# Order of loads, flushes and far updates in the recurrence of a four-layer graph kernel on one core

## The chip, the core and the metric

The kernel runs on one NeuronCore of a Trainium2 chip. A core has five engines, each with its own queue of instructions in program order: TensorE (PE, with its weight loads PEld), VectorE (DVE), ScalarE (ACT), GpSimd (POOL) and SyncE (SP, which here only issues DMA transfers). The metric is the device time of one execution in microseconds; lower is better.

## The reference

The input is x of 64 graphs x 256 nodes x 256 features and a weighted adjacency matrix per graph. Four layers follow each other, each of the form x = layernorm(x + layer(x, adj)). The change is in layer 0, a recurrence over the nodes, in which all 64 graphs go side by side:

```python
d = jnp.sum(adj, axis=-1)
dinv = jnp.where(d != 0, 1.0 / jnp.where(d != 0, d, 1.0), 0.0)
norm_adjT = jnp.swapaxes(adj, 1, 2) * dinv[:, :, None]

def step(h, i):
    x = jnp.take(h_e, i, axis=1)
    row = jnp.take(norm_adjT, i, axis=1)
    x_par = jnp.einsum('bj,bjd->bd', row, h)
    iou = x @ W_ioux.T + b_ioux + x_par @ W_iouh.T + b_iouh
    r, z = jnp.split(iou, 2, axis=1)
    r, z = (jax.nn.sigmoid(r), jax.nn.sigmoid(z))
    hc = jnp.tanh(x @ W_coux.T + b_coux + x_par * r @ W_couh.T + b_couh)
    h_new = z * x_par + (1.0 - z) * hc
    h = jax.lax.dynamic_update_slice(h, h_new[:, None, :], (0, i, 0))
    return (h, None)
h_out, _ = jax.lax.scan(step, h_e, jnp.arange(n))
```

Node i needs the sum x_par over all nodes j: for j < i with the new states h, for j >= i with the old ones, which are x itself. The 256 steps cannot run side by side. Layers 1 to 3 are a graph convolution, a masked attention and a masked attention with eight heads, done graph by graph.

## The kernel before

**Setup.** The function `_recurrence` first computes, for the first 128 nodes, the part of x_par that comes from old states (the loop over `g` in steps of `GB` = 8 graphs, products in `x_product`, VectorE's copies, stores into the DRAM tensor `Us` in `x_out`). Weights are loaded and turned in between. The input tiles `xX` are loaded from ACT's queue (L139), `xA` from SP's (L138). Then the pools of setup are given back, and the pools `stream`, `work` and `ps` take their memory: a tile of those pools waits until the old users of its memory are done. After this come the first S table (`chain_S(0)`), the raw table for late sums (`late_load(0)`), the first x (`load_x`, SP) and the first three blocks of sums (`sums_in`, ACC from `Us`).

**A node.** The main loop runs over the nodes n, written out by hand: the order of the calls is the order on each engine, and no scheduler moves them. i = n % 32 is the row in a block of T = 32 nodes, p = n % 8 the place in a group of U = 8. A tile of 128 x 128 holds a state: 2 feature halves x 64 graphs on the partitions. The chain of a node is: transpose of xp on TensorE and ScalarE's copy into xpT; the products of r and z with xpT (`h_part`, L615); ScalarE's sigmoid rs (L839); transpose and product into rT; the products of c; tanh (L876); then on VectorE zcc (L878) and the next xp (L881). `state` (L661, L663) writes the new state twice, into PSUM (`keep`) and into SBUF (`hs`).

**How a new state reaches later nodes.** Each node's sum lies in the tile ACC of its group. The state of node n-1 must be added, times an entry of S, to the nodes up to the end of the next group:
- near targets by VectorE, one instruction each (`push`, L640). They stand in a list sorted by target; one or more for node n+1 come first, then up to 5 (`push(5)`), then up to 3 late in the node (`push(3)`, ahead of zcc);
- the last `FAR[p]` targets by GpSimd (`push_far`, a product into the tile `far`, L678, and a sum into ACC, L682), in the same node. At place 0 `behind` adds two more such pairs of 4 targets for the group after;
- everything further away by matrix products over many states at once. `late` (L531) reads the ring `Hw` of the last 64 states and goes through the DRAM tensor `Lb` into `late_sb`, which GpSimd adds at places 6 and 7 (L891). `early` (L424) reads states and adjacency from DRAM (`Hs`, `A`) and goes through `Es` into `early_sb`, added at places 3 and 4 (L833). `x_side` does the same for old states of the second 128 nodes, through `Us`.

GpSimd also makes `ready` (L820), which the next xp needs. Results of these products leave PSUM by ScalarE copies that stand in the list `copies`: one is taken at a node's start and two at its end (`next_of`). The output tile `ub` (copies xu and eu, L256) has two buffers in `stream`.

**Transfers.** All transfers in the loop are issued by SP, in this order in a node: states into the ring (`into_ring`, places 4 to 7, two states of two transfers each); two loads from a list ordered by rank (`next_load`, places 0 to 3); the transfers that earlier steps put on this node (`transfers`: stores to `Us`, `Es`, `Lb`, the receipt of `late_sb`); `early_sb` (place 0), ACC (place 1), x (place 2); the flush of ring rows to the DRAM tensor `Hd` (at rows 10 and 16); and what `degrees` does for the next block. `degrees` is a generator that is advanced at 14 given rows: four loads of 4 x 2 adjacency rows, two reductions on VectorE (L304) after each, then the inverse and the spread to `dinv`.

Of the kernel before, what the change touches and what calls it, by code (L numbers as in the profile page):

```python
# [9 lines left out]
F32 = mybir.dt.float32  # L10
# [9 lines left out]
P = 128  # L20
# [50 lines left out]
def _recurrence(tc, ident, Hd, x, adj, W_ioux, b_ioux, W_iouh, b_iouh, W_coux, b_coux, W_couh, b_couh, wide, then):  # L71
# [27 lines left out]
    XB = 4  # L99
    NG = B // 4  # L100
    HB = B // 2
    FAR = (2, 4, 4, 4, 4, 4, 3, 4)

    with ExitStack() as ctx:
        const = ctx.enter_context(tc.tile_pool(name="r_const", bufs=1))
# [467 lines left out]

        def load_x(a):

            xq = stream.tile([P, U // 2, D], F32, tag="xq", name=f"xq_{a}")
            for h in range(2):
                at = a * U + h * U // 2
                nc.sync.dma_start(xq[h * B:(h + 1) * B], x[:, at:at + U // 2, :])
            return xq  # L580

        def flip_x(a, e, xq):
# [89 lines left out]

        def push_far(j, hs, first, count):

            acc, s = cell(j, first, count)
            tmp = work.tile([P, 4, P], F32, tag="far", name=f"far_{j}_{first}", bufs=1)
            shape = [P, count, P]
            nc.gpsimd.tensor_mul(  # L678
                tmp[:, 0:count, :], hs.unsqueeze(1).to_broadcast(shape),
                s.unsqueeze(2).to_broadcast(shape),  # L680
            )
            nc.gpsimd.tensor_add(acc, acc, tmp[:, 0:count, :])  # L682

        tables = {k: {} for k in range(NB)}
        sums = {}
# [9 lines left out]
        with tc.tile_pool(name="r_first_ps", bufs=4, space=bass.MemoryType.PSUM) as xps:  # L695
            for g in range(0, B, GB):
                A, Xs = first_in.pop(0)
                nc.gpsimd.tensor_mul(
                    A[:, 0], A[:, 0], tri.unsqueeze(1).to_broadcast([P, GB, P])
                )  # L700
                for n in range(0, GB, 4):
                    ub = fst.tile([P, 4, D], F32, tag="ub", name=f"xu_{g}_{n}")
                    for e in range(0, 4, 2):
                        pb = xps.tile([P, 2, D], F32, tag="x", name=f"xp_{g}_{n}_{e}")
                        for q in range(2):
                            b = n + e + q
                            x_product(
                                pb, q, [A[:, jc, b, :] for jc in range(2)],
                                [Xs[jc][:, b, :] for jc in range(2)],
                            )  # L710
                        nc.vector.tensor_copy(ub[:, e:e + 2, :], pb)
                    x_out(0, g + n, ub)
                if g + 2 * GB < B:
                    first_in.append(first_load(g + 2 * GB))
                if g == 0:
                    load_weights()
                if g == 3 * GB:
                    turn_weights()
                if g == 2 * GB:
                    deg = fst.tile([P, T // 2], F32, name="deg_0", bufs=1)  # L720
                    nc.vector.tensor_reduce(deg, rows_0, AX.X, ALU.add)
                    inverse(deg, fst.tile([P, T // 2], F32, name="deg0_0", bufs=1))
                    dinv_from(deg, 0)
# [3 lines left out]
        work = ctx.enter_context(tc.tile_pool(name="r_work", bufs=2))  # L727
        ps = ctx.enter_context(tc.tile_pool(name="r_ps", bufs=1, space=bass.MemoryType.PSUM))

        tables[0]["Sd"] = chain_S(0)  # L730
        tables[0]["An"] = late_load(0)
        xq = {a: load_x(a) for a in range(2)}
        for a in range(3):
            sums_in(a)
        for e in range(2):
            flip_x(0, e, xq[0])
# [7 lines left out]
                x_part(G, 0, kc, gates)  # L744

        keep = ps.tile([P, 4, P], F32, tag="keep", name="keep")
        xp = new("xp", 0)
        nc.vector.tensor_scalar(xp, sums[0][:, 0, :], dinv[:, 0:1], None, ALU.mult)

        zcc = hs = None  # L750
        late_side = background = None
        behind = []
        x_left = x_side()
# [18 lines left out]
        for now in range(N):  # L772
# [4 lines left out]

            xpT = flip(xp, "xpT", n)
            next_of(copies, n)

            far = []
            if n:

                assert all(j == n - 2 for _, j in pushes)
                hs = state(n - 1)
                end = min((n - 1) // U * U + 2 * U, N)
                to = list(range(n + 1, end))
                near = to[:len(to) - min(FAR[p], len(to) - 1)] if to else []
                far = to[len(near):]
                pushes += [(m, n - 1) for m in near]  # L790
                pushes.sort()
                if p == 0:

                    behind = [(n - 1, hs, m, 4) for m in range(end, min(end + U, N), 4)]

                if p > 3 or n >= N - U:
                    for _ in range(min(2, len(ring_in))):
                        into_ring()
# [23 lines left out]
                    dinv[:, n + 1:n + 2].to_broadcast([P, P]),  # L822
                )
            push(5)
            if far:
                push_far(n - 1, hs, far[0], len(far))
            if behind:
                push_far(*behind.pop(0))
            if p in (3, 4):
# [35 lines left out]
            if not last:  # L865
                Sd = tables[kk]["Sd"][:, ii:ii + 1]
                v = keep[:, 3, :]
                nc.vector.scalar_tensor_tensor(v, zx, Sd, ready, ALU.mult, ALU.add)
                push(3)
                for kc in range(2):  # L870
                    x_part(rc, n + 1, kc, slice(0, 2))
                z = ps.tile([P, P], F32, tag="z", name=f"z_ps_{n + 1}")
                nc.scalar.copy(z, bias_z)
                for kc in range(2):
                    x_part(z, n + 1, kc, 2)
# [1 line left out]
            zcc = new("zcc", n, 1)  # L877
            nc.vector.tensor_mul(zcc, zc, c)  # L878
            if not last:
                xp = new("xp", n + 1)  # L880
                nc.vector.scalar_tensor_tensor(xp, zcc, Sd, v, ALU.mult, ALU.add)  # L881
            for _ in range(2):
                next_of(copies, n)
            if p < 4:
                for _ in range(2):
                    next_load(n)

            if p in (6, 7) and n + 8 - p in sides:
                half = slice(0, U // 2) if p == 6 else slice(U // 2, U)
                part = sums[n // U + 1][:, half]  # L890
# [8 lines left out]
                sums_in(n // U + 3)  # L899
            if p == 2 and n // U + 2 < N // U:  # L900
                xq[n // U + 2] = load_x(n // U + 2)
            if i == 10:
                flush(n - 26, n - 10)
            if i == T // 2:
                state_out(n - 1, hs)
                flush(n - T // 2, n - 1)
# [19 lines left out]
        while ring_in:  # L926
            into_ring()
# [618 lines left out]
```

## Time and profile before

| what | value |
|---|---|
| median of 3 runs | 3314.0 us (3300.75, 3314.0, 3314.47) |
| the profiled execution, own time | 3314.75 us |
| its span | 3313.0 us |
| mean granted TensorE clock | 0.973 |
| TensorE busy | 3077.3 us, 93% of the span |
| VectorE / ScalarE / GpSimd busy | 2630.6 / 1834.0 / 1925.8 us |
| share of TensorE in the chain that ended last | 79% |
| L640, near updates on VectorE | 1712, 478.6 us busy |
| L682 and L678, far updates on GpSimd | 313 each, 372.4 and 304.9 us busy |
| L839, the sigmoid rs on ScalarE | 256, 277 ns each |

The span is the time from the first to the last instruction of the profiled execution. Busy times of different engines overlap. In the timeline a row is: start and length in us, engine, line, operation, output and inputs, shape, count, and in brackets the idle time before it with what ended it. In a table of waits a row is: engine and line, what it waited for, total us, times, longest.

### The profile page before, as it was taken

The page shows a single profiled execution, that of the slowest core. Times are in us where ns is not written, and L with a number is a line of the kernel's source. Part 1 is how long each engine was busy: PE and PEld are TensorE (multiplying, and loading weights), DVE is VectorE, ACT ScalarE, POOL GpSimd, SP SyncE. Part 2 cuts the span into 40 slices and gives each one's busy share as a digit, 9 for nine tenths or more (in the row PEclk, how much of TensorE's full clock was granted, in tenths as well). Part 3 has the DMA queues.
Part 4 walks back from the last instruction along what each step waited for, and adds up shares of the span by engine and source line. Part 5 has one row for each costly group of instructions (what it writes and reads, how often), then busy time and mean ns, then how long its engine had stood idle before and what let it go on. Part 6 is the DMA issues. An engine that isn't in the chain of part 4 may idle for free.

```text
span 3313.0 us, 80062 instructions
## 1 busy us (share of the span) xinstructions
PE 3077.3 (93%) x28332; PEld 2275.4 (69%) x28332; DVE 2630.6 (79%) x7511; ACT 1834.0 (55%) x4690; POOL 1925.8 (58%) x2230
## 2 busy tenths in 40 slices
PE   4798979999989998977999999999999999999997
PEld 3565656565555555545888888888888888888885
DVE  3476767887777878865888888888888888888885
ACT  0154535554545544534666666666666666666664
POOL 2366667777667878843555555555555555555543
PEclk8899989999999999998999999999999999999999
DMA  9865557686867675424333333333333333333310
GB/s 295 250 163 132 156 144 178 157 194 166 202 166 179 152 180 136 118 58 94 76 77 78 78 78 78 76 81 77 76 79 79 77 78 77 78 77 78 77 43 20
DMA packets 806730, 385.73 MB, mean 116 GB/s; under 512 B 525260, under 2 KB 774232, under 8 KB 802648
## 3 DMA queue, kind: packets, MB, share of 16 engines
q1 hardware_dynamic: 788632, 363.66, 45.3%
q10 hardware_dynamic: 17696, 16.91, 1.6%
q8 instruction: 227, 3.72, 0.5%
q14 instruction: 175, 1.43, 0.1%
HBM read 261.75 MB, written 99.61 MB: 109 GB/s over the span
## 4 chain that ended last, share of the span: by engine, by line
PE 79%; DMA 8%; DVE 7%; issue 2%; SPq 2%; ACT 2%; POOL 1%; DVEq 0%; ACTq 0%; POOLq 0%
PE mm L1023 14%; PE rc L615 7%; PE rc L607 4%; PE s L1249 4%; PE mm_3v L1023 4%; PE mm_2f L1023 4%; PE late L531 3%; PE mm_2v L1023 3%; PE mm_3f L1023 3%; PE mm_t L1023 3%; PE mm_g L1023 3%; PE mm_2w L1023 3%; PE mm_2s L1023 3%; PE o L1284 3%; DVE ACC L640 3%; PE z_ps L615 2%
## 5 line engine op out<-in xcount | busy, mean ns | idle before, releaser
L1261 POOL TENSOR_TENSOR p3s<-p 128x256 f32<-128x256 f32 x512 | 359.2, 735 | 271.2 <-ACT p L1259 271.0
L640 DVE SCALAR_TENSOR_TENSOR ACC<-keep,S,ACC 128x128 f32<-128x128 f32 x1712 | 478.6, 343 | 14.2 <-POOL ACC L891 8.6
L1023 PE MATMUL mm<-xT,weights 128*128 128x256 f32 x2048 | 484.1, 385 | 2.7 <-ACT xT L1139 2.7
L1023 PEld LDWEIGHTS mm<-xT,weights 128*128 128x128 f32 x2048 | 386.3, 191 | 80.2 <-ACT xT L1139 28.8
L682 POOL TENSOR_TENSOR ACC<-ACC,far 128x384 f32<-128x384 f32 (+1 forms) x313 | 372.4, 1190 | 24.5
L1258 DVE TENSOR_TENSOR p<-s,neg 128x512 f32<-128x512 f32 x512 | 317.7, 683 | 85.6 <-PE s L1249 85.6
L979 ACT ACTIVATE y<-y,shift,rstd 128x256 f32<-128x256 f32 x512 | 279.7, 596 | 156.3 <-DVE shift L977 156.2
L1259 ACT ACTIVATE p<-p 128x512 f32<-128x512 f32 x512 | 307.1, 629 | 3.5 <-DVE p L1258 3.0
L678 POOL TENSOR_TENSOR far<-hs,S 128x384 f32<-128x384 f32 (+1 forms) x313 | 304.9, 974 | 4.7
L820 POOL TENSOR_TENSOR ready<-ACC,dinv 128x128 f32<-128x128 f32 x255 | 102.2, 401 | 316.1 <-DVE ACC L640 315.6
L607 PE MATMUL rc<-WxT,xqT 128*64 128x256 f32 x2048 | 276.2, 392 | 0.0
L971 POOL TENSOR_TENSOR rstd<-rstd,mhalf 128x2 f32<-128x2 f32 x256 | 173.8, 697 | 133.4 <-DVE rstd L970 131.6
L1298 DVE RECIPROCAL rT<-o 128x256 f32<-128x256 f32 x128 | 223.7, 1748 | 0.0
L967 DVE BATCH_NORM_STATS2 st<-y 128x6 f32<-128x256 f32 x512 | 209.6, 409 | 12.6 <-POOL y L1160 9.7
L615 PE MATMUL rc<-WhT,xpT 128*64 128x128 f32 x2048 | 170.7, 288 | 43.1 <-ACT xpT L624 40.3
L839 ACT ACTIVATE rs<-rc 128x128 f32<-128x128 f32 x256 | 70.9, 277 | 247.5 <-PE rc L615 247.5
L1160 POOL TENSOR_TENSOR y<-y,g 128x512 f32<-128x512 f32 x64 | 81.3, 1270 | 215.2 <-ACT g L1157 195.3
L615 PE MATMUL rc<-WhT,rT 128*64 128x128 f32 x2048 | 172.9, 291 | 33.6 <-DVE rT L843 33.1
L615 PEld LDWEIGHTS rc<-WhT,rT 128*64 128x64 f32 x2048 | 109.5, 139 | 131.8 <-DVE rT L843 111.7
L1171 ACT ACTIVATE qk<-mm,weights 128x256 f32<-128x256 f32 x256 | 107.3, 470 | 161.2 <-PE mm L1023 159.6
L615 PEld LDWEIGHTS rc<-WhT,xpT 128*64 128x64 f32 x2048 | 107.9, 137 | 124.2 <-ACT xpT L624 112.9
L531 PE MATMUL late<-Hw,An 64*32 64x256 f32 x3840 | 165.4, 396 | 25.6 <-DMA A<-in_adj_dram 9.9
(168 smaller groups left out, 7239.3 us busy)
## 6 DMA issues: line engine op xcount, KB each, us to landing
xX<-in_x_dram ACTq DMA_DIRECT2D x16, 1024.0 KB
Us<-xu SPq DMA_DIRECT2D x64, 256.0 KB
xq<-in_x_dram SPq DMA_DIRECT2D x64, 256.0 KB
ACC<-Us SPq DMA_DIRECT2D x32, 512.0 KB
Es<-eu SPq DMA_DIRECT2D x64, 256.0 KB
early_sb<-Es SPq DMA_DIRECT2D x32, 512.0 KB
xin<-in_x_dram SPq DMA_DIRECT2D x64, 256.0 KB
ad<-in_adj_dram SPq DMA_DIRECT2D x64, 256.0 KB
```

What stands on the lines that cost most here:

```text
L531: nc.tensor.matmul(pb[g][q * T:(q + 1) * T, e, :], An[rows, b].rearrange("p u s -> p (u s)"), Hw[rows, b, :], start=True, stop=True,)
L607: nc.tensor.matmul(G[o * B:(o + 1) * B], xqT[a, i // 2][:, i % 2, kc, h * B:(h + 1) * B], WxT[:, kc, o, gates], start=False, stop=False, s ...
L615: nc.tensor.matmul(G[o * B:(o + 1) * B], hT[:, kc * B:(kc + 1) * B], WhT[:, kc, o, g], start=False, stop=(kc == 1), skip_group_check=True,)
L640: nc.vector.scalar_tensor_tensor(acc[:, 0, :], keep[:, j % 2, :], s, acc[:, 0, :], ALU.mult, ALU.add)
L678: nc.gpsimd.tensor_mul(tmp[:, 0:count, :], hs.unsqueeze(1).to_broadcast(shape), s.unsqueeze(2).to_broadcast(shape),)
L682: nc.gpsimd.tensor_add(acc, acc, tmp[:, 0:count, :])
L979: nc.scalar.activation(y[:, c, :], y[:, c, :], AF.Identity, bias=shift[:, c:c + 1], scale=rstd[:, c:c + 1],)
L1023: nc.tensor.matmul(pm[:, c, :], lhsT[:, k, c * P:(c + 1) * P], rhs[:, k, :], start=(k == 0), stop=(k == 1),)
L1258: nc.vector.tensor_add(p, s_ps[i], self.neg3)
L1259: nc.scalar.activation(p, p, AF.Exp, scale=ISQ)
L1261: nc.gpsimd.tensor_add(both, p[:, 0, :], p[:, 1, :])
L1298: nc.vector.reciprocal(rT, o_ps[:, 1, :])
```

## The change

Five things change, all in `_recurrence`:
- **Far targets.** `FAR` grows by one at places 0 to 4. The far update of a state now stands one node later, and its first two products (three at place 4) are made by ScalarE, one activation (copy with a scale) per target, between the node's xpT copy and its sigmoid; GpSimd makes the other products and the sum. The tile `far` holds five targets and still has one buffer.
- **Near targets.** The late `push(3)` is now `push(2)`; the tile xp has one buffer instead of two.
- **Loads.** The two `next_load` calls of places 0 to 3 stand at the end of the node, after every other transfer.
- **Flush and degrees.** The first flush of a block is at row 8 instead of 10, with the rows that fit. The degree generator is advanced twice at row 3 and no longer at row 12, so its second, third and fourth loads stand at rows 3, 11 and 17 instead of 8, 12 and 17.
- **Setup.** The first two x tiles lie in the pool `blk` and are loaded from ACT's queue during the loop over `g`. After the loop, the first ACC load stands first. A one-column sigmoid on ScalarE follows, then the raw table and S.

```diff
-    FAR = (2, 4, 4, 4, 4, 4, 3, 4)
+    FAR = (3, 5, 5, 5, 5, 4, 3, 4)
...
-            xq = stream.tile([P, U // 2, D], F32, tag="xq", name=f"xq_{a}")
+            if a < 2:
+                xq = blk.tile([P, U // 2, D], F32, tag="early", name=f"xq_{a}")
+            else:
+                xq = stream.tile([P, U // 2, D], F32, tag="xq", name=f"xq_{a}")
             for h in range(2):
                 at = a * U + h * U // 2
-                nc.sync.dma_start(xq[h * B:(h + 1) * B], x[:, at:at + U // 2, :])
+                (nc.scalar if a < 2 else nc.sync).dma_start(
+                    xq[h * B:(h + 1) * B], x[:, at:at + U // 2, :]
+                )
...
         def push_far(j, hs, first, count):
 
+            scale_far(j, hs, first, count, 0)()
+
+        def scale_far(j, hs, first, count, begun):
+
             acc, s = cell(j, first, count)
-            tmp = work.tile([P, 4, P], F32, tag="far", name=f"far_{j}_{first}", bufs=1)
-            shape = [P, count, P]
-            nc.gpsimd.tensor_mul(
-                tmp[:, 0:count, :], hs.unsqueeze(1).to_broadcast(shape),
-                s.unsqueeze(2).to_broadcast(shape),
-            )
-            nc.gpsimd.tensor_add(acc, acc, tmp[:, 0:count, :])
+            tmp = work.tile([P, 5, P], F32, tag="far", name=f"far_{j}_{first}", bufs=1)
+            for e in range(begun):
+                nc.scalar.activation(tmp[:, e, :], hs, AF.Copy, scale=s[:, e:e + 1])
+
+            def finish():
+                if begun < count:
+                    shape = [P, count - begun, P]
+                    nc.gpsimd.tensor_mul(
+                        tmp[:, begun:count, :], hs.unsqueeze(1).to_broadcast(shape),
+                        s[:, begun:count].unsqueeze(2).to_broadcast(shape),
+                    )
+                nc.gpsimd.tensor_add(acc, acc, tmp[:, 0:count, :])
+
+            return finish
...
+                if g == B - 3 * GB:
+                    xq = {a: load_x(a) for a in range(2)}
...
+        sums_in(0)
+        warm = work.tile([P, P], F32, tag="ready", name="warm", bufs=1)[:, 0:1]
+        nc.vector.memset(warm, 0.0)
+        nc.scalar.activation(warm, warm, AF.Sigmoid)
+        tables[0]["An"] = late_load(0)
         tables[0]["Sd"] = chain_S(0)
-        tables[0]["An"] = late_load(0)
-        xq = {a: load_x(a) for a in range(2)}
-        for a in range(3):
+        for a in range(1, 3):
             sums_in(a)
...
+            add_far = far and scale_far(*far, min(3 if p == 4 else 2, far[-1]))
...
-                near = to[:len(to) - min(FAR[p], len(to) - 1)] if to else []
-                far = to[len(near):]
+                near = to[:len(to) - max(0, min(FAR[p], len(to) - 2))]
+                far = (n - 1, hs, to[len(near)], len(to) - len(near)) if near != to else []
...
             push(5)
-            if far:
-                push_far(n - 1, hs, far[0], len(far))
+            if add_far:
+                add_far()
...
-                push(3)
+                push(2)
...
-            if p < 4:
-                for _ in range(2):
-                    next_load(n)
-
...
-            if i == 10:
-                flush(n - 26, n - 10)
+            if i == U:
+                flush(n - 24, n - 8)
...
-                if i in (0, 2, 3, 8, 10, 11, 12, 15, 16, 17, 20, 21, 23, 24):
+                for _ in range((0, 2, 3, 3, 8, 10, 11, 15, 16, 17, 20, 21, 23, 24).count(i)):
                     next(background, None)
...
+            if p < 4:
+                for _ in range(2):
+                    next_load(n)
```

More of the change, by code (lines that the diff above doesn't have):

```diff
@@ L746, in _recurrence @@
         keep = ps.tile([P, 4, P], F32, tag="keep", name="keep")
-        xp = new("xp", 0)
+        xp = new("xp", 0, 1)
         nc.vector.tensor_scalar(xp, sums[0][:, 0, :], dinv[:, 0:1], None, ALU.mult)
-        zcc = hs = None
+        zcc = hs = far = None
         late_side = background = None
@@ L879, in _recurrence @@
             if not last:
-                xp = new("xp", n + 1)
+                xp = new("xp", n + 1, 1)
                 nc.vector.scalar_tensor_tensor(xp, zcc, Sd, v, ALU.mult, ALU.add)
```

## The prediction

> **What bounds the kernel now.** I read the stage windows first, then the timeline of layer 0, then the table of waits in that stage. The windows cut the span at the first and last copy of `xpT` (one per node):
>
> ```profile
> 0.00:139.15 139.15, 77.38 (x311) 61.71 (x312) 38.07 (x62) 2.99 (x5) 28.73 (x22) 0.83 0.98 290
> 139.15:1471.45 1332.30, 1216.39 (x15952) 773.78 (x15950) 1017.76 (x3595) 658.72 (x2183) 964.47 (x1054) 0.97 0.64 157
> 1480.00:3313.00 1833.00, 1777.91 (x12034) 1436.18 (x12034) 1571.49 (x3844) 1171.06 (x2497) 932.31 (x1152) 0.98 0.32 74
> ```
>
> The columns are the length, then busy PE, PEld, DVE, ACT, POOL, then clock, DMA share and GB/s. Setup is bound by DMA (0.98 busy). The recurrence is 255 steps of one serial chain. Layers 1 to 3 (1833 us) are not touched, so I leave them alone.
>
> From the starts of the 256 `xpT` copies I took each node's length. The medians for places p = 0 to 7 of a group of 8 are 5.56, 4.81, 4.81, 5.15, 4.64, 5.20, 4.64 and 4.63 us; over 255 steps these sum to 1257 of the 1332 us. The rest is in few nodes: the 33 that lie over 0.6 us above their median hold 93 us together. So there are two things to gain: the length of an ordinary node, and the stalls.
>
> An ordinary node of place 3 in the timeline:
>
> ```profile
> 850.67 0.36 DVE L868 SCALAR_TENSOR_TENSOR keep<-keep,Sd,ready 128x128 f32<-128x128 f32 x1
> 851.06 1.00 DVE L640 SCALAR_TENSOR_TENSOR ACC<-keep,S,ACC 128x128 f32<-128x128 f32 x3
> 851.18 0.26 ACT L876 ACTIVATE rc<-rc 128x128 f32<-128x128 f32 x1 [0.31 <-PE rc L615]
> 851.98 0.28 DVE L878 TENSOR_TENSOR zcc<-zc,rc 128x128 f32<-128x128 f32 x1
> 852.69 0.33 PE L622 MATMUL xpT_ps<-ident,xp 128*128 128x128 f32 x1 [0.32 <-DVE xp L881]
> ```
>
> The tanh (L876) is ready at 851.44, but zcc starts at 851.98, behind three updates of ACC on the same engine: VectorE decides here. PE then waits 0.32 us. At places 0, 1 and 4 to 7 the chain of waits runs through PE pieces nearly without a gap, so a faster VectorE gains nothing there.
>
> The stalls, from ScalarE's table of waits in the recurrence (total, times, longest in us), and then one of them in its timeline:
>
> ```profile
> ACT rs L839 <- PE rc L615: 246.7, 254, 4.2
> ACT xu L256 <- DMA Us<-xu: 18.2, 5, 10.5
> ACT eu L256 <- DMA Es<-eu: 12.2, 4, 4.2
> ```
>
> ```profile
> 302.95 0.58 ACT L256 COPY eu<-early 128x512 f32<-128x512 f32 x1 [4.19 <-DMA Es<-eu]
> 303.43 0.27 ACT L624 COPY xpT<-xpT_ps 128x128 f32<-128x128 f32 x1
> ```
>
> The tile `ub` (written by the copies xu and eu) has two buffers. A copy waits until the store from its buffer has landed, and the next node's `xpT` stands behind it on ScalarE. After such a gap the eight rc matmuls take 1.12 us in the chain of waits, not 0.59, so the next node is long too.
>
> Setup's end, SP and others:
>
> ```profile
> 125.53 0.91 SPq L220 DMA_DIRECT2D Us<-xu  x2
> 128.74 2.44 SPq L579 DMA_DIRECT2D xq<-in_x_dram  x4
> 131.22 1.71 SPq L316 DMA_DIRECT2D ACC<-Us  x3
> 135.02 0.58 ACT L256 COPY xqT<-xqT_ps 128x512 f32<-128x512 f32 x1 [7.61 <-DMA xq<-in_x_dram]
> 138.30 0.28 DVE L748 TENSOR_SCALAR xp<-ACC,dinv 128x128 f32<-128x128 f32 x1 [12.80 <-DMA ACC<-Us]
> 139.44 1.28 ACT L839 ACT_TABLE_LOAD   x1
> ```
>
> Everything waits from 125.5 to 128.74 for the last `Us` store to land; then x, ACC and the raw table are fetched in a row.
>
> **What the Trainium skill says.** "TensorE: Matmul & The Clock Gate", Part 1, says that PE falls to half rate after an idle window of about 3.4 us and needs about as long busy to come back. The trace agrees: 1.12 against 0.59 us above, after 4.19 us of idle. "DMA: Bandwidth & Descriptors", Issuing engines are not separate DMA queues, says that queues of SP and ACT run on the same 16 engines. So x fetched sooner by ACT is not free: it takes the time of other setup loads. The trace shows both queues sharing 0.98. "ScalarE: Activation LUTs", What ACT_TABLE_LOAD costs, prices an activation at 186 ns plus 0.833 ns per column, 93 ns more for a pointer operand, and 93 ns of overlap back to back. For 128 columns this gives an estimate of 0.39 us alone and 0.29 in a row. Without the pointer it is 0.29, and the trace has 0.277 for L839.
>
> **The change, part by part.** All is summed against the profiled execution, 3314.75 us (span 3313.0, 1.75 around it), 0.75 above the median of the three runs.
>
> *Setup.* The x loads (four of 256 KB) go out early on ACT's queue. One MB at 350 GB/s (the rate in 110 to 118 us) is 3 us of a full DMA stage: the `Us` landing moves from 128.74 to at most 131.7. After it: ACC is first in the queue, the two xqT copies follow at once (PE's flips wait for no load any more), then PE's x parts, 1.91 + 0.85 as in the chain now, then the xpT transpose and copy. That is 0.6 + 2.8 + 0.5, so xpT starts about 4 to 5 us after the landing, where now it is 10.4. ACC alone should land in 4 (now 7 from its issue, behind 1 MB of x). So 5.5 less at most 3, with 0.3 more from the table load, which moves into idle time. In the built order ScalarE's warm-up stands ahead of the last two x loads of the products; if its memory is not free it holds them by up to 1 us. I take -3; the ends are -5.5 and +1.
>
> *Ordinary nodes.* FAR moves five targets in eight nodes from VectorE to POOL, and the third update at L868's end goes: one of 0.29. Place 3 gains 0.30 in the 16 nodes after a degree reduction (5.15), until PE bounds at about 4.8, and 0.14 in the other 16 (4.94): 4.8 + 2.2. Place 2 is 4.81 with PE at about 4.77: 32 x 0.04 = 1.3. The reduction that goes from row 11 to 8 frees place 4 of row 12 (4.76 to 4.64): 8 x 0.12 = 1. Sum 9. Ends: -14 and -3.
>
> *ScalarE's scales.* Two per node, three at place 4, stand between xpT and the sigmoid rs. ScalarE waits 246.7/254 = 0.97 us there. Two cost 0.58 to 0.78, three 0.87 to 1.17. So they hide, except perhaps at place 4 (0.96 idle; loss up to 0.2 x 32 = 6) and place 0 (0.83 idle). Place 1 has an lb copy ahead (xpT ends 838.28, lb 838.76, scales about 839.3, rs now 839.54): hidden. I take 0; ends 0 and +8. If the cover goes, each 0.1 us is 3 us per place.
>
> *POOL.* A far node was 1.04 + 1.28 (L678, L682, 4 targets); now the product is of 3 (0.83, between the rows of 0.61 and 1.04) and the sum of 5 (1.55, the line through 0.73 and 1.28). About the same. The deferral by one node relieves place 1, where far and `behind` met: ready 0.40, 0.40 + 1.00, 1.04 + 1.28, gaps 0.3, together 4.4 of 4.81.
>
> *`ub` waits.* Nodes 15, 23-24, 29-31, 38-39, 46, 55-56, 61-63, 70-71 and 78 hold 43 us over their medians. Loads last means that x is fetched a little later, and the built order of xu and eu copies changes. I listed for each `ub` tile the node of its first copy and the node of the last copy into the buffer it takes: now nine tiles come within one node, four of them in the same node. After: six (nodes 15, 21, 30, 47, 53, 62), all one node apart. One-node cases now cost 2 (place 7), 7 (place 5, with the node behind) and 3 (place 6): 2 x 2 + 2 x 7 + 2 x 3 = 24 remain. -19; ends -35 and 0.
>
> *SP's order otherwise.* The other 50 us (nodes 18, 51, 88, 112, 143-144, 200 and smaller) hang on late `Lb`, `Hw` or late sums. At node 143 a flush (895.3), a raw load (2.84 us to issue) and `Lb` (4.17 and 3.17) follow each other, and POOL gets `late_sb` 9.3 us late. Now the flush leaves at row 8, `Lb` stands ahead of its node's loads and the degree rows come one to five nodes sooner. But the forced raw loads and the flush at row 16 stay, and SP still issues every transfer. Nothing in the trace prices this; between 0 and -40, I take a third, -17.
>
> Sum: 3314.75 - 3 - 9 - 19 - 17 = 3266.75, so 3267.
>
> **Rivals.** *Stalls only move.* The transfers are the same bytes, and other copies come close together. Then only setup and nodes gain: 3314.75 - 12 = 3303. For: each stall is a chance meeting in a queue. Against: four same-node reuses are gone by construction.
>
> *Nearly all stalls go.* -3 - 9 - 35 - 40 gives 3228. For: the last block has almost none. Against: six close reuses and the row 16 flush remain.
>
> *Slower: the single `far` buffer.* ScalarE now writes `far` ahead of its sigmoid, so in order it waits until POOL's sum of the node before has read it. At place 1 POOL must end 5.5 us after place 0's start, and the scale comes at about 6.2; at place 2 the slack is 0.5. If POOL runs late, the wait lands on rs and delays the chain. A mean of 0.31 us per node is 80 us, so 3267 + 80 = 3347. From 0.19 us per node (48/255) it eats the gain. Against: my sums leave slack at each place, though with two early parts (last two blocks) only some 0.1 at place 6.
>
> **Numbers.** Likely case (3245 to 3297) 0.50; nearly all stalls gone 0.20; stalls only move 0.18; slower 0.12. What counts as no change is within 0.5%, 3297 to 3331. So faster 0.70, same 0.18, slower 0.12. The range 3230 to 3306 leaves out most of the slower case and the end of the best one.
>
> **What will show it.** First xpT at 133 to 138. Place 3 at about 4.85 with two updates ahead of zcc. ScalarE's wait before rs down to about 0.3 us, with no wait of the scales for POOL; if they wait, the slower case is on. The waits of xu and eu for their stores down from 30 to below 20 us. Node 143 and 55 near their medians. An unchanged total above the medians would make the stall part wrong.

## The result and the profile after

| | before | after |
|---|---|---|
| median (range) | 3314.23 us (3300.75 to 3318.02, 4 runs) | 3274.21 us (3268.15 to 3276.55, 4 runs) |
| ratio, 95% interval | | 0.9884 [0.9853, 0.9915] |
| span of the profiled execution | 3313.0 us | 3274.8 us |
| mean granted TensorE clock | 0.973 | 0.974 |

The kernel is 40 us faster; the forecast was 47. First the stage windows of the kernel after, cut as those of before at the first and last copy of `xpT` (columns: length, then busy PE, PEld, DVE, ACT, POOL, then clock, DMA share, GB/s):

```profile
0.00:135.18 135.18, 78.65 (x311) 62.52 (x312) 38.03 (x63) 3.10 (x7) 28.45 (x22) 0.84 0.98 296
135.18:1431.84 1296.66, 1204.71 (x15952) 770.16 (x15950) 973.13 (x3444) 815.38 (x2716) 922.39 (x1049) 0.98 0.67 161
1440.00:3274.80 1834.80, 1782.69 (x12038) 1439.22 (x12036) 1573.64 (x3846) 1170.93 (x2497) 930.79 (x1152) 0.98 0.32 74
```

Setup is 4.0 us shorter, the recurrence 35.6 (1332.30 to 1296.66). The rest of the span, from the last `xpT` to the end, is 1.4 longer. ScalarE's busy time in the recurrence rose by 157 us (658.72 to 815.38): it has taken over the scales. DVE's fell by 45.

The same from the starts of the `xpT` copies, node by node:

| us | before | after |
|---|---|---|
| median, places 0 to 3 | 5.56, 4.81, 4.81, 5.15 | 5.96, 4.69, 4.69, 4.78 |
| median, places 4 to 7 | 4.64, 5.20, 4.64, 4.63 | 4.63, 5.22, 4.64, 4.64 |
| nodes over 0.6 us above their median | 33, holding 93.4 | 23, holding 62.9 |
| first 80 nodes together | 445.5 | 415.1 |
| the 175 after them | 886.8 | 881.6 |
| all nodes of place 0 together | 206.5 | 225.8 |
| of these, seven at row 8 (40, 72, ... 232), above 5.44 each | 7.0 | 23.9 |
| all nodes of places 1 to 3 | 478.5 | 452.8 |
| all nodes of places 4 to 7 | 647.3 | 618.1 |

So the gain sits in the first 80 nodes. After them nearly nothing is left, although the ordinary nodes are shorter there as well: something took it back. The sums by place say where: places 1 to 3 gained 25.7 us and places 4 to 7 gained 29.2, and place 0 lost 19.3. With 4.0 from setup and 1.4 lost after the recurrence these make up the 38.2 us between the two spans.

**An ordinary node.** Place 3 in the timeline of the kernel after (start, length, engine, line, operation, shape, count, and in brackets the idle time before it):

```profile
818.32 0.36 DVE L890 SCALAR_TENSOR_TENSOR keep<-keep,Sd,ready 128x128 f32<-128x128 f32 x1
818.71 0.74 DVE L645 SCALAR_TENSOR_TENSOR ACC<-keep,S,ACC 128x128 f32<-128x128 f32 x2
818.86 0.26 ACT L898 ACTIVATE rc<-rc 128x128 f32<-128x128 f32 x1 [0.34 <-PE rc L620]
819.36 0.28 DVE L900 TENSOR_TENSOR zcc<-zc,rc 128x128 f32<-128x128 f32 x1
820.08 0.33 PE L627 MATMUL xpT_ps<-ident,xp 128*128 128x128 f32 x1
```

Two updates of ACC stand before zcc, not three. The tanh (L898) ends at 819.12 and zcc starts 0.24 later; before it was 0.54. PE's transpose now shows no idle time in brackets. The scales lie before the sigmoid, two of them at place 3 and three at place 4:

```profile
815.82 0.69 ACT L687 ACTIVATE far<-hs,S 128x128 f32<-128x128 f32 x2
816.91 0.28 ACT L861 ACTIVATE rs<-rc 128x128 f32<-128x128 f32 x1 [0.39 <-PE rc L620]
...
820.61 0.98 ACT L687 ACTIVATE far<-hs,S 128x128 f32<-128x128 f32 x3
821.67 0.28 ACT L861 ACTIVATE rs<-rc 128x128 f32<-128x128 f32 x1
```

After two scales ScalarE still waits 0.39 us for PE; after three it goes on at once. They hide.

**The waits.** ScalarE's table of waits in the recurrence of the kernel after (what waited, for what, total us, times, longest), to be set beside the one of before:

```profile
ACT rs L861 <- PE rc L620: 86.5, 192, 4.2
...
ACT xu L256 <- DMA Us<-xu: 6.9, 2, 4.5
...
ACT xu L256 <- DMA Es<-eu: 3.2, 2, 2.5
...
ACT far L687 <- POOL ACC L696: 0.8, 2, 0.4
```

The waits of xu and eu for stores fell from 30.4 us in nine to 10.1 in four. The wait before rs fell from 246.7 to 86.5: filled with scales. The scales waited for GpSimd 0.8 us in all, so the slower rival (the single `far` buffer) is out. TensorE's table has the opposite sign. First the row of before, then that of after:

```profile
PE late L531 <- DMA Hw<-hs: 7.3, 5, 2.4
```

```profile
PE late L531 <- DMA Hw<-hs: 21.5, 11, 4.4
```

The late products now wait for states written to the ring `Hw`, for 14 us more. All waits of `late` together, whatever they are put down to, rose from 23.7 to 34.9 us. Node 104 (row 8), TensorE and then SP in the timeline of the kernel after:

```profile
671.28 0.33 PE L863 MATMUL rT_ps<-ident,rs 128*128 128x128 f32 x1
675.65 1.11 PE L531 MATMUL late<-Hw,An 64*32 64x256 f32 x16 [4.05 <-DMA Es<-eu]
676.69 1.12 PE L620 MATMUL rc<-WhT,rT 128*64 128x128 f32 x8
```

```profile
641.72 10.40 SPq L269 DMA_DIRECT2D raw<-in_adj_dram  x1
...
660.09 6.68 SPq L676 DMA_DIRECT2D Hw<-hs  x8
666.87 1.46 SPq L436 DMA_DIRECT2D Es<-eu  x2
668.42 2.76 SPq L676 DMA_DIRECT2D Hw<-hs  x4
```

The node starts at 669.9. SP issues one transfer after the other and is still at the ring writes at 671.2, when TensorE wants them. The bracket names `Es`, but the `late` product reads the ring, and at node 136 the same wait is put down to `Hw`. TensorE idles 4.05 us, and the eight rc matmuls after it take 1.12 us instead of 0.66.

All the kernels of this study can be looked at together. At place 0 the `late` product needs the ring writes of the group before. For each of 30 nodes of place 0 (8, 16, ... 240) in the profiled executions of 14 kernels (before, after and the twelve experiments) I took the start of the last issue of a ring write against the node's own start:

| last ring write issued, against the node's start | nodes | node's length: shortest, median, longest (us) |
|---|---|---|
| more than 3 us ahead | 237 | 5.43, 5.50, 8.01 |
| 2 to 3 us ahead | 68 | 5.44, 6.05, 9.09 |
| 1 to 2 us ahead | 37 | 6.23, 7.23, 9.52 |
| 0 to 1 us ahead | 31 | 7.33, 9.41, 12.26 |
| after it | 47 | 9.86, 11.64, 13.79 |

The later the last ring write, the longer the node: from 5.5 us to nearly 12 over some four us of lateness. This is a pattern over unlike kernels and not an experiment: no run moved the ring writes alone, and busy DMA engines could lengthen both. Less than 3 us ahead were 7 of the 30 nodes in the kernel before and 16 after; after the node's start 3 (112, 144, 200) before and 5 (104, 120, 136, 144, 200) after. The seven nodes at row 8 alone lost 16.9 us and node 0 (below) 2.6; together that is about what place 0 lost; its other nodes gained and lost in equal parts.

**Setup.** Its end in the timeline of the kernel after:

```profile
130.65 1.28 SPq L316 DMA_DIRECT2D ACC<-Us  x3
130.71 1.07 ACT L256 COPY xqT<-xqT_ps 128x512 f32<-128x512 f32 x2 [1.05 <-DMA Us<-xu]
...
134.32 0.29 DVE L769 TENSOR_SCALAR xp<-ACC,dinv 128x128 f32<-128x128 f32 x1 [6.62 <-DMA ACC<-Us]
...
135.18 0.27 ACT L629 COPY xpT<-xpT_ps 128x128 f32<-128x128 f32 x1 [3.40 <-PE xpT_ps L627]
...
135.92 1.12 PE L620 MATMUL rc<-WhT,xpT 128*64 128x128 f32 x8
```

The last `Us` store lands at 130.65, 1.9 later than before. ACC follows in 3.7 us, without x ahead of it. The first `xpT` is 4.0 us sooner. But here the first eight rc matmuls take 1.12 us, and node 0 takes 7.48 us where it took 4.88: 2.6 of the 4.0 go back.

How much of this is the change can be read from all 14 kernels, of which four have the old setup and ten the new. From the landing of the last `Us` store to the first `xpT` it took 10.2 to 10.9 us with the old setup and 4.3 to 4.7 with the new, as the change intends. The landing itself came at 124.8 to 128.7 us with the old and at 129.3 to 132.5 with the new; that fits x loads that share the DMA engines with the stores. So the first `xpT` starts at 135.7 to 139.2 us and at 133.8 to 137.0: in the mean 2.3 us sooner, not 4.0. Node 0 took 4.9 us in all four old kernels; in the new ones it took about 7.5 us in six and 4.3 in four. The wait of TensorE just ahead does not tell these apart (1.77 us in a kernel with 4.33, 0.69 in one with 7.49). What decides stays open.

### The profile page after: what moved, and what is told of

Read it like the earlier page. It is cut to its first block, busy times and chain, and to the rows that moved or that the text cites. A ratio compares the mean times of both kernels' runs of the same rounds, so it can differ in the third digit from the quotient of the medians.

```text
span 3274.8 us, 80656 instructions
## 1 busy us (share of the span) xinstructions
PE 3071.4 (94%) x28332; PEld 2275.9 (69%) x28332; DVE 2587.5 (79%) x7361; ACT 1990.7 (61%) x5224; POOL 1881.9 (57%) x2226
## 4 chain that ended last, share of the span: by engine, by line
PE 82%; DMA 7%; DVE 6%; issue 2%; SPq 2%; POOL 1%; ACT 1%; ACTq 0%; DVEq 0%; POOLq 0%
PE mm L1044 14%; PE rc L620 7%; PE rc L612 5%; PE s L1270 4%; PE late L531 4%; PE mm_3v L1044 4%; PE mm_2f L1044 4%; PE mm_2v L1044 3%; PE mm_3f L1044 3%; PE mm_t L1044 3%; PE mm_g L1044 3%; PE mm_2s L1044 3%; PE mm_2w L1044 3%; PE o L1305 3%; PE z_ps L620 2%; PE z_ps L612 2%
## 5 line engine op out<-in xcount | busy, mean ns | idle before, releaser
L696 POOL TENSOR_TENSOR ACC<-ACC,far 128x640 f32<-128x640 f32 (+2 forms) x312 | 412.8, 1323 | 69.8 <-ACT far L687 26.1
L645 DVE SCALAR_TENSOR_TENSOR ACC<-keep,S,ACC 128x128 f32<-128x128 f32 x1561 | 436.8, 343 | 13.0 <-POOL ACC L909 8.2
L692 POOL TENSOR_TENSOR far<-hs,S 128x384 f32<-128x384 f32 (+1 forms) x310 | 222.0, 716 | 4.7
L531 PE MATMUL late<-Hw,An 64*32 64x256 f32 x3840 | 166.3, 402 | 35.7 <-DMA Hw<-hs 21.5
L620 PE MATMUL rc<-WhT,xpT 128*64 128x128 f32 x2048 | 170.9, 288 | 25.7 <-ACT xpT L629 24.5
L687 ACT ACTIVATE far<-hs,S 128x128 f32<-128x128 f32 x534 | 183.7, 397 | 3.1 <-POOL ACC L696 0.8
```

The source lines that it names most:

```text
L531: nc.tensor.matmul(pb[g][q * T:(q + 1) * T, e, :], An[rows, b].rearrange("p u s -> p (u s)"), Hw[rows, b, :], start=True, stop=True,)
L620: nc.tensor.matmul(G[o * B:(o + 1) * B], hT[:, kc * B:(kc + 1) * B], WhT[:, kc, o, g], start=False, stop=(kc == 1), skip_group_check=True,)
L645: nc.vector.scalar_tensor_tensor(acc[:, 0, :], keep[:, j % 2, :], s, acc[:, 0, :], ALU.mult, ALU.add)
L692: nc.gpsimd.tensor_mul(tmp[:, begun:count, :], hs.unsqueeze(1).to_broadcast(shape), s[:, begun:count].unsqueeze(2).to_broadcast(shape),)
```

## The experiments

**One part undone at a time.** The experiments ran in three groups, and the kernel before was measured beside each (medians 3308.23, 3313.34 and 3310.24 us); across groups the ratios to it are what can be compared. My theory stood on the order of the `ub` copies, with the far updates second; the rivals were that SP's order by itself, or the flush and the degree rows, bring the rest. In the diffs, a plus is what the experiment has and the kernel named lacks.

The loads, against the kernel after: ahead of the transfers again.

```diff
             for _ in range(2):
                 next_of(copies, n)
+            if p < 4:
+                for _ in range(2):
+                    next_load(n)
...
-            if p < 4:
-                for _ in range(2):
-                    next_load(n)
         state(N - 1)
```

> The changed kernel, with the two loads of a node put back ahead of the node's other transfers. Theory (the loads' place sets which copies into ub follow each other, and so the stalls): the copies stand as in the kernel before, the waits of xu and eu for their stores come back from 11 to about 30 us, and the time rises by 20 to 30 us over the changed kernel, to 3295 to 3305. Rival (the stalls moved by chance, the gain is in the far updates and the flush): within 8 us of the changed kernel's 3274.

Measured: 3327.48 us, ratio to before 1.006 [1.0043, 1.0077]: slower than the kernel before, and 53 us over the kernel after (58 by the ratios), more than the 20 to 30 expected. ScalarE's waits in its recurrence, and one of them in its timeline:

```profile
ACT xu L256 <- DMA Us<-xu: 18.6, 5, 10.9
ACT eu L256 <- DMA Es<-eu: 17.1, 4, 5.5
```

```profile
301.54 0.59 ACT L256 COPY eu<-early 128x512 f32<-128x512 f32 x1 [4.17 <-DMA Es<-eu]
302.02 0.27 ACT L629 COPY xpT<-xpT_ps 128x128 f32<-128x128 f32 x1
302.18 0.70 ACT L687 ACTIVATE far<-hs,S 128x128 f32<-128x128 f32 x2
```

Nine waits as in the kernel before, and behind each not only `xpT` but now also the scales. GpSimd's row, in this kernel and then in the kernel after:

```profile
POOL ACC L696 <- ACT far L687: 51.3, 31, 8.2
```

```profile
POOL ACC L696 <- ACT far L687: 26.1, 17, 3.4
```

So with the far part a stall of ScalarE reaches GpSimd's sums as well. That can't be why the old load order costs 53 us here and only 37 in the kernel before (both below): the kernel with the far part alone has the old load order too, and GpSimd waits there nearly as long:

```profile
POOL ACC L691 <- ACT far L682: 48.6, 34, 8.1
```

Yet that kernel is 12 us faster than the kernel before. All that this experiment has on top of it is the new setup and the new flush and degree rows, and by the ratios (1.006 and 0.9964) these go with 32 us more. GpSimd's waits for `late_sb` (24.2 us against 14.7) and TensorE's for the ring (14.6 against 5.9) are longer as well. Which of the three parts it is, with the old load order, was not tried.

The far updates, against the kernel after: `FAR`, `push_far`, `push(3)` and the two xp buffers of before.

```diff
-    FAR = (3, 5, 5, 5, 5, 4, 3, 4)
+    FAR = (2, 4, 4, 4, 4, 4, 3, 4)
...
-            add_far = far and scale_far(*far, min(3 if p == 4 else 2, far[-1]))
...
-                push(2)
+                push(3)
```

> The changed kernel, with FAR, the far updates on GpSimd alone and in the same node, and the late push of three put back. Theory (VectorE decides at places 1 to 3): medians of places 1 to 3 return to 4.81, 4.81 and 5.15, which is 0.6 us a group or 20 us, so 3290 to 3296; stalls as in the changed kernel. Rival (VectorE's work is hidden, the nodes got shorter because fewer stalls slow TensorE): 3270 to 3280.

Measured: 3283.51 us, ratio 0.9931 [0.9914, 0.9948]. Against the kernel after that is 9 us in the medians and 16 in the ratios (0.0047 of 3314). The medians of places 1 to 3 went back to 4.81, 4.81 and 4.94.

The flush and the degree rows, against the kernel after:

```diff
-            if i == U:
-                flush(n - 24, n - 8)
+            if i == 10:
+                flush(n - 26, n - 10)
...
-                for _ in range((0, 2, 3, 3, 8, 10, 11, 15, 16, 17, 20, 21, 23, 24).count(i)):
+                if i in (0, 2, 3, 8, 10, 11, 12, 15, 16, 17, 20, 21, 23, 24):
```

> The changed kernel, with the flush back at row 10 and the degree rows at 0, 8, 12 and 17. Theory (the rows at place 3 stand ahead of the ring writes on SP's queue, which is full at places 4 to 7, so that the late product at row 8 of blocks 3, 4 and 6 waits about 6 us for the ring): those three stalls go, others at rows 15 to 20 come back in part; 3258 to 3276. Rival, the prediction's step (the flush away from Lb removes the stalls of nodes 143 and 55): 3285 to 3295.

Measured: 3266.39 us, ratio 0.9884 [0.9867, 0.9901], the same ratio as the kernel after. This part gains nothing that can be resolved. The time lies in the range expected, but the three stalls that were to go stayed. The last ring writes at nodes 104, 136 and 200 are issued 0.5 to 0.7 us ahead of the nodes here, where the kernel after has them 0.65 to 1.2 us late; these nodes still take 9.2 to 10.3 us.

The setup, against the kernel after: x from SP into `stream` after the loop, ACC behind it, no one-column sigmoid.

```diff
-            if a < 2:
-                xq = blk.tile([P, U // 2, D], F32, tag="early", name=f"xq_{a}")
-            else:
-                xq = stream.tile([P, U // 2, D], F32, tag="xq", name=f"xq_{a}")
+            xq = stream.tile([P, U // 2, D], F32, tag="xq", name=f"xq_{a}")
...
-                if g == B - 3 * GB:
-                    xq = {a: load_x(a) for a in range(2)}
```

> The changed kernel, with x loaded after the setup loop on SP's queue, ahead of ACC, and no early sigmoid. Theory: the first xpT comes 4 us later, but TensorE is warm then and node 0 is 2.6 us shorter: 1 to 3 us over the changed kernel, 3275 to 3277. Rival, the prediction's best end: 5.5 us, 3279 to 3280.

Measured: 3274.23 us, ratio 0.9898 [0.9881, 0.9914], with the first `xpT` at 139.03. The 4 us sooner are not seen in the time.

**One part alone.** The loads alone are the diff of the first experiment in reverse, made to the kernel before; the far updates alone likewise.

> The kernel before with nothing but the two loads put last in the node. Theory: it holds most of the gain, 30 to 45 us below the kernel before, 3265 to 3280, as the far updates give 9 and the flush and degree rows cost 8. Rival (the parts need each other): at most 15 us below.

Measured: 3276.78 us (before beside it 3313.34), ratio 0.9889 [0.9856, 0.9922]. This is nearly the whole gain.

> The kernel before with nothing but the far and near updates changed. Theory: places 1 to 3 get shorter by 0.6 us a group, 20 us in the medians, of which stalls take half: 5 to 15 us below the kernel before. Rival (with loads in front, the faster nodes run into the same transfers): no gain, within 5 us of the kernel before.

Measured: 3301.64 us, ratio 0.9964 [0.9951, 0.9977]: 12 us. ScalarE's waits for stores out of `ub` stay (xu 18.9, eu 14.3 us).

**What in the place of the loads matters?** A load at the end of a node does two things. SP issues it behind the node's other transfers. And it comes after the call `early_ahead(n)`, which queues the loads of the next early work, so that a load can go out in the node that queues it and not a node or more later; that changes when the early work starts, and so which xu and eu copies follow each other into the two buffers of `ub`. Two kernels separate the two. The first has the loads after nearly all transfers (only those of the degrees and tables follow) but ahead of the queueing, against the kernel after:

```diff
+            if p < 4:
+                for _ in range(2):
+                    next_load(n)
             early_ahead(n)
...
-            if p < 4:
-                for _ in range(2):
-                    next_load(n)
         state(N - 1)
```

> The changed kernel, with the two loads behind the node's transfers but ahead of the step that queues new early loads (so a load queued in a node goes out a node later, as in the kernel before). SP's order is nearly that of the changed kernel; the built order of the ub copies is that of the kernel before (nine close reuses). Theory (the copy order makes the stalls): about the time of the kernel with the loads undone, 3315 to 3330, with xu and eu waits of about 30 us. Rival (the loads' place in SP's queue counts): 3272 to 3285.

Measured: 3340.33 us, ratio 1.0079 [1.0054, 1.0104], with the nine close reuses of `ub` of the old order. Its ScalarE waits:

```profile
ACT eu L256 <- DMA Es<-eu: 28.3, 4, 8.8
ACT xu L256 <- DMA Us<-xu: 12.5, 5, 4.5
```

The second has the loads early in SP's queue, but the queueing ahead of them:

```diff
             for _ in range(2):
                 next_of(copies, n)
+            early_ahead(n)
+            if p < 4:
+                for _ in range(2):
+                    next_load(n)
...
-            early_ahead(n)
...
-            if p < 4:
-                for _ in range(2):
-                    next_load(n)
```

> The changed kernel, with the loads ahead of the node's transfers as before, but with the step that queues early loads ahead of them. SP's order is nearly that of the kernel before; the copy order is that of the changed kernel (six close reuses). Theory: near the changed kernel, 3275 to 3290, xu and eu waits near 11 us. Rival: 3315 to 3330.

Measured: 3264.77 us, ratio 0.9847 [0.9814, 0.988], with the six close reuses of the new order. Its ScalarE waits:

```profile
ACT xu L256 <- DMA Us<-xu: 4.9, 2, 2.9
ACT xu L256 <- DMA Es<-eu: 0.2, 1, 0.2
```

The first pair of lines holds 40.8 us, the second 5.1; the two kernels are 75 us apart. With the first experiment and the kernel after, every pairing is there: with the queueing first the ratio is 0.9847 for early loads and 0.9884 for loads last, with the loads first it is 1.006 and 1.0079. So the loads' place in SP's queue goes the other way, if it does anything (the intervals overlap in both pairs), and the queueing first brings 65 to 70 us at either place. What pays is the order of queueing against loading, one call moved by some lines.

**Is it the wait for the store?** If the copy order costs because a copy waits for the store of the tile before it, a sooner store must win part of it back with the old order. Against the first experiment (loads undone), with the stores from `ub` one node sooner:

```diff
-                                lambda n, b=g, ub=ub: at_step(n + 1, lambda: x_out(1, b, ub))
+                                lambda n, b=g, ub=ub: at_step(n, lambda: x_out(1, b, ub))
...
-                    (lambda n: at_step(n + 1, store)) if t % 2 else None,
+                    (lambda n: at_step(n, store)) if t % 2 else None,
```

> The kernel with the loads undone, with the stores to Us and Es from ub issued in the node of their last copy, not one node later. The copy order stays that of nine close reuses; only the time that a reuse waits for its store is shorter. Theory (waiting for the store is what the copy order costs): 20 to 40 us below 3327, so 3287 to 3307, xu and eu waits from 36 to below 15 us. Rival (the copy order counts for another reason, such as which early products lie in which node): 3320 to 3330.

Measured: 3292.23 us, ratio 0.9948 [0.9929, 0.9968], 35 us below the same kernel with the stores of before, and the first 80 nodes fell from 456.1 to 422.3 us. The copy order is unchanged. The waits for the stores:

```profile
ACT xu L256 <- DMA Us<-xu: 12.3, 2, 6.9
ACT eu L256 <- DMA Es<-eu: 9.6, 4, 4.8
```

They came to 21.9 us from 35.7, where I had expected less than 15. So a shorter wait for the store wins back some 35 of the 53 us with the copy order as it was. The edit also moves the stores in SP's queue, so it does not change the wait alone; but the same move of the stores costs time below, and the seven row-8 nodes changed little here (22.3 to 18.7 us over 5.44 each). A third buffer for `ub`, which would take the wait away altogether, was not tried.

**Putting it together.** The queueing ahead, the loads early, and the flush and degree rows of before:

```diff
             for _ in range(2):
                 next_of(copies, n)
+            early_ahead(n)
+            if p < 4:
+                for _ in range(2):
+                    next_load(n)
...
-            if i == U:
-                flush(n - 24, n - 8)
+            if i == 10:
+                flush(n - 26, n - 10)
```

> The version with the queueing step ahead and the loads early in the node, with flush and degree rows as in the kernel before. Theory (the two effects add): 3265 - 8 = 3257, the best so far. Rival (they remove the same stalls at row 8): 3263 to 3268.

Measured: 3258.02 us (before beside it 3310.24), ratio 0.985 [0.983, 0.987]. This is the lowest median of all, but the ratio can't be told from the 0.9847 of the kernel with the new flush. Its profiled execution was the fastest of its four (3247.17 us). The seven row-8 nodes hold only 3.1 us over 5.44 each in it, with the last ring writes at 104, 136 and 200 issued 1.8 to 3.2 us ahead. With the new flush and degree rows (the kernel with the queueing ahead and the loads early) it was 0.86 and 0.11 us ahead and 0.93 late, and the nodes took 9.8 to 12.8 us. The same kernel with the stores one node sooner as well:

> The same with the stores from ub in the node of their last copy. Theory: the xu waits that are left (5 us, nodes 15 and 47, with the node behind some 7) go, 5 us less than without, about 3252. Rival (SP then waits at the store with the ring writes behind it): 3 to 10 us more than without.

Measured: 3273.52 us, ratio 0.9883 [0.9866, 0.9901], 15 us slower than without. ScalarE's waits for stores are down to 0.4 us, so the sooner store does what it should. TensorE's waits in this kernel, and then in the one without sooner stores:

```profile
PE late L531 <- DMA Hw<-hs: 21.5, 9, 4.5
...
PE late L531 <- DMA Es<-eu: 8.7, 3, 4.4
```

```profile
PE late L531 <- DMA Hw<-hs: 17.4, 6, 6.0
```

The ring writes come late again: at node 136, 0.75 us after the start where it was 2.73 ahead. A store issued in the node of its copy waits for the copy, at the head of SP's queue, and what stands behind it waits too. SP's own waits at these stores, with sooner stores and then without:

```profile
SPq L436 <- ACT eu L256: 39.4, 18, 3.2
SPq L220 <- ACT xu L256: 19.0, 13, 3.2
```

```profile
SPq L436 <- ACT eu L256: 6.9, 8, 1.7
SPq L220 <- ACT xu L256: 2.6, 4, 1.0
```

So SP is held 58.4 us at the stores where it was held 9.5. That this alone makes the ring writes late was not tested by itself.

Last, the degree rows alone undone, with the new flush kept, against the kernel after:

```diff
-                for _ in range((0, 2, 3, 3, 8, 10, 11, 15, 16, 17, 20, 21, 23, 24).count(i)):
+                if i in (0, 2, 3, 8, 10, 11, 12, 15, 16, 17, 20, 21, 23, 24):
```

> The changed kernel, with the degree rows alone put back to 0, 8, 12 and 17 (the flush stays at row 8). Theory (the rows at place 3 delay the ring writes): as good as with both undone, 3262 to 3270. Rival (the flush at row 8 is what costs): 3272 to 3278.

Measured: 3277.10 us, ratio 0.9889 [0.9868, 0.9909], not better than the kernel after. My theory that the second degree load at row 3 brings the stalls at row 8 fell. The time lies in the rival's range, but that the flush costs is not shown by it, as undoing both left the ratio where it was (0.9884). Which transfer makes SP late there stays open. The 10.40 us issue of a raw table ahead of node 104 is not it alone: the best kernel has one of 10.68 us there, and the kernel before one of 8.34.

## Why the prediction came near, point by point

- **Setup, -3.** The first `xpT` came 4.0 us sooner, within the ends given, and the landing 1.9 later, where at most 3 were foreseen. The steps after the landing were forecast well: 4 to 5 us, and 4.3 to 4.7 in all ten kernels that have them. Missing was the slow first node, which gave 2.6 back here. The part is worth about 1 us in the traces and nothing in the time.
- **Ordinary nodes, -9.** Undoing the far part cost 9 us in the medians, 16 in the ratios; alone it gave 12. By the medians, places 1 to 3 gained 32 x (0.12 + 0.12 + 0.37) = 19.5: place 3 as forecast (4.78 for 4.85), place 2 three times its 0.04. I had called places 0 and 1 bound by TensorE, where a faster VectorE gains nothing; place 1 gained 0.12 a node. Place 0 got longer by 0.40 in the median, which I did not foresee: its ring writes come later, as below.
- **The scales, 0.** Right: two took 0.69 us (estimate 0.58 to 0.78), three 0.98 (0.87 to 1.17), and ScalarE's wait before rs covered them. They waited 0.8 us in all for GpSimd, so the case of 3347 fell with the sign and size of its wait.
- **`ub` waits, -19.** The mechanism was right, the size too small. The nine and six close reuses came as listed, but of the six only nodes 15 and 47 stalled. They and the nodes behind them held 9.7 us over their medians, not 24. Node 53 of the list lay 4.0 us over its median too, but its copy did not wait: TensorE had waited 2.42 us for the adjacency `A` of an early product. All nodes that wait for `ub` before or after, with the nodes behind, held 43.1 us before and 16.4 after: 27 gained where 19 were booked. The term had priced every close reuse that is left like one of before.
- **"SP's order otherwise", -17. This is the step that failed.** It took a third of the remaining stalls as the gain of loads standing last, of the flush away from `Lb` and of the degree rows. The two kernels that separate queueing and place show no gain from the place (3264.77 us early, against 3274.21 last), and undoing the flush and degree rows left the ratio at 0.9884. The seven nodes that it named (18, 51, 88, 112, 143, 144, 200) did fall, from 38.5 us over their medians to 14.6, but others came (104, 119, 120, 136, 184): after the 80th node all stalls together held 39.8 us before and 39.3 after. There the rival "stalls only move" was right. Place 0 took 19.3 us more (206.5 to 225.8), most of it in nodes whose ring writes are issued late. I had listed the wait ("late `Hw`") among the causes of the stalls, and read its sign the wrong way.

  Even node 143, the example of this term (9.4 us over its median before, 0.1 after), moved for another reason. It lies 9.1 to 10.8 us over in the five kernels with the old order of queueing and loading, new flush rows or loads last among them, and 0.0 to 3.5 in the nine with the new order, whatever their flush rows and loads. So the order of queueing does more than change the copies into `ub`. Ahead of the flush that I blamed, a load of states for the early work had held SP's queue in the kernel before, which the prediction left out:

```profile
881.42 12.13 SPq L269 DMA_DIRECT2D Hs<-Hd  x1
893.60 1.66 SPq L579 DMA_DIRECT2D xq<-in_x_dram  x2
895.30 1.04 SPq L650 DMA_DIRECT2D Hd<-Hw  x2
```

  That this load is what delayed `Lb` fits the order of the queue, but was not tested by itself.
- **The sum.** It came within 7 us since errors cancel, which is luck. Places 4 to 7, where the `ub` stalls sit, gained 29.2 us where 19 were booked, and places 1 to 3 gained 25.7, stalls included; place 0 took back about as much as SP's order was booked to bring. A close total is no proof of its parts.
- **What would show it.** The marks came true: setup, place 3, the waits of xu and eu below 20, nodes 143 and 55. But node 143 did so for another reason than the one given. The wait before rs is 86.5/192 = 0.45 us (over all 255 nodes 0.34; forecast 0.3). The total above the medians fell from 93.4 to 62.9 us.
- **A reading.** The 4.19 us ahead of the slow rc matmuls are ScalarE's wait; TensorE, whose idle time the argument is about, had stood idle for 3.75 us there.

## What to carry to other kernels

Where two producers share an output tile with two buffers, list which copy goes into whose buffer, node by node, for both program orders, before anything about transfers is guessed: one call moved by some lines was worth more here than any other part. Price a stall of an in-order engine with what follows it, not by its own idle time: with the stores sooner, ScalarE's waits for them fell by 13.8 us and the time by 35. And where one engine issues all transfers in order, measure for the transfer that a node needs how far ahead of the node it is issued: here nodes with the last write issued after their start were twice as long as those with it 3 us ahead (11.64 and 5.50 us).

## What the runs showed of the hardware that was not expected

- One transfer can hold SP's queue for about 10 us: the raw table load took 10.40 us to issue at 641.72 in the kernel after and 10.68 in the best kernel, and the same line 0.35 and 0.58 us elsewhere. It is not a matter of this load alone: a load of states took 12.13 us at 881.42 in the kernel before, and a load of x 9.87 at 1139.12 in the kernel after. An issue of a ring write takes 0.7 to 0.8 us (eight in 6.68, four in 2.76). What a long issue waits for the trace doesn't say.
- After 4.05 us of idle TensorE ran the `late` and rc products more slowly (eight rc matmuls 1.12 us against 0.66). A stalled node so costs more than the wait it shows.
